# Cross attention on one core: product 7 of y in blocks in five batches, and T4 by a ScalarE copy and accumulating DMAs

## The chip, the core and the metric

The kernel runs on one NeuronCore of a Trainium2 chip. It is one program for five engines, each with its own queue that runs in order: TensorE (PE, matmuls; its weight loads are listed as PEld), VectorE (DVE), ScalarE (ACT), GpSimd (POOL) and SyncE (SP, which here only issues DMAs). ACT and POOL also issue DMAs. The metric is the device time of one execution in microseconds, as the median of several; the profile is of one further execution.

## The reference

For each of B = 8 batches, with x1 and x2 of 512 channels and 1024 positions, all in float32:

```
q = einsum('bcn,dc->bnd', x1, Wq) + bq
k = einsum('bcn,dc->bdn', x2, Wk) + bk[:, None]
v = einsum('bcn,dc->bdn', x2, Wv) + bv[:, None]
attn = softmax(einsum('bnd,bdm->bnm', q, k), axis=2)
out = einsum('bcm,bnm->bcn', v, attn) + x1
```

The queries and keys have 64 channels (d), the values 512.

## The kernel before

The kernel never forms v. It uses that v·attnᵀ = Wv·(x2·E)/den + bv, where E holds the exponentials of the scores (less a maximum for each query) and den their sums. So each batch has two large products: **y = x2·E** (512 x 1024 times 1024 x 1024) and **o = Wv·y** (512 x 512 times 512 x 1024).

**Seven products in place of eight.** Each large product is cut into 2 x 2 quarters and done by the Strassen-Winograd scheme: from the quarters of the left side (x2, names `a`; 11, 12, 21, 22) come four sums S1 to S4, from those of the right side (E, or y) come T1 to T4, and seven quarter products, numbered 1 to 7, replace eight. For y, a quarter product is 8 matmuls of 128x512 (two row halves j, four steps of 128 positions), and the profile counts two records for each float32 matmul. `multiply` does one whole (matmuls at L322), adding in PSUM onto chains in two pairs of banks, `a0`/`a1` and `c0`/`c1`. After products 1, 6 and 5 of y ScalarE copies the state of the chain from PSUM to SBUF (L333; tiles `u1`, `u6`, `u5`), because several results need it. The order of the products is 1, 2, 6, 5, 7, 3, 4. Then `evict_y` makes the four quarters of y: it adds bank and tile (step 1, L481) and multiplies with the reciprocal sums `rden` (step 2, L483).

**Products in blocks.** Some of the seven are themselves done by the same scheme one level down: product 2 (`multiply_2`, in b > 0), 3 and 4 (`multiply_onto`, in all batches). `inner_left` (L354, four additions of 128x256 on VectorE, tiles `aI`) and `inner_right` (L365, four of 128x512, tiles `eI`) make the inner sums; `inner_product` (L372) does one of seven block products with 2 matmuls of 128x256, four records. The block products that go straight into the bank of the outer chain are 2, 4 and 3. The others run in a chain of their own in a bank of the pool `ps_s`, which has two buffers and which the scores use as well; ScalarE copies what is needed to `d` and `v` (L381, 128x256). `complete` (L441) adds v to the second half of d; then d is added where the outer product belongs: for product 4 to `u6` (L451), for product 3 into y12 while bank a is read (L461).

**The order.** The order of every queue is written out by hand: `period(s, n, nn, nnn)` is one batch `s`, and into it are laid the next batch's scores, maxima and exponentials (`n`) and the queries and keys of the one after (`nn`). What matters here, as the program issues it in the middle of a period:

1. `multiply_2` on PE; on VectorE the sum over the exponentials' tiles of the second half, POOL's all-reduce of it (`total`, L235) and a small DMA (L237), then product 2's additions (L416).
2. `sum_t4` (two additions of 128x1024, L271, on VectorE), S4, T3 (L271 again), and product 6 on PE.
3. The right blocks of product 4 from T4 and the left blocks of product 3.
4. The next batch's scores for the first half of the queries (L190; copies to SBUF at L197 and L199), the queries of the batch after (L148), then the maxima over them on VectorE (`fold`, L210, L225) and POOL's all-reduce of the maximum (`highest`, L230).
5. `shares`: the reciprocals (L243), spread by two DMAs of POOL (L245, L247).
6. Product 5; the maximum is subtracted (`lower`, L258, VectorE), the exponential taken (L262, ScalarE), a first tile copied (L539) and the other three added by accumulating DMAs of POOL (`add_tile`, L531).
7. Product 3's right blocks, product 7, product 4's left blocks, product 3, and the readings of the banks: y22 from bank c, y12 from bank a.
8. The scores of the second half (the third of four tiles goes into bank a, `ps_sa`), the keys, product 4, and then o with its seven products.

Batch b = 6 has no queries of a later batch at step 4, and the last batch, b = 7, has no next batch at all. Tiles with one tag share one buffer: a new tile may be written when the old one has no readers left.

The sums of the scheme are set by short tables, for the left side in `left_sums` and `LEFT`, for the right side in `right_sums` and `RIGHT`:

```
"S1": ("21", "22", ALU.add),
"S2": ("S1", "11", ALU.subtract),
"S3": ("11", "21", ALU.subtract),
"S4": ("12", "S2", ALU.subtract),
x, y = {"T1": ("12", "11"), "T2": ("22", "T1"), "T3": ("22", "12"), "T4": ("21", "T2")}[k]
```

Of the kernel before, what the change touches and what calls it, by code (L numbers as in the profile page):

```python
# [15 lines left out]
def kernel(  # L16
# [8 lines left out]
    bv: bass.AP,  # L25
    out: bass.AP,
):

# [69 lines left out]
    def left_sums(a, *ks):  # L100

        for k in ks:
            x, y, op = {
                "S1": ("21", "22", ALU.add),
                "S2": ("S1", "11", ALU.subtract),
                "S3": ("11", "21", ALU.subtract),
                "S4": ("12", "S2", ALU.subtract),
            }[k]
            nc.vector.tensor_tensor(a["21" if k == "S3" else k], a[x], a[y], op)
            if k == "S3":  # L110
                a["S3"] = a["21"]
# [155 lines left out]

    def right_sums(t, k):

        x, y = {"T1": ("12", "11"), "T2": ("22", "T1"), "T3": ("22", "12"), "T4": ("21", "T2")}[k]  # L270
        nc.vector.tensor_tensor(t[k], t[x], t[y], ALU.subtract)  # L271

    def open_t(s):
        for n in ("T1", "T2"):
# [3 lines left out]
        s.t["T3"] = s.t["12"]  # L278

    def sum_t4(s):  # L280
        s.t["T4"] = sb.tile([P, MH, H], F32, tag="eT4", name=f"eT4_{s.b}")
        sum_e(s, "T4")

    def sum_e(s, *ks):
        for i in (0, 2):
            part = {n: v[:, i : i + 2, :] for n, v in s.t.items()}
            for k in ks:
                right_sums(part, k)
# [18 lines left out]
        4: ("22", "T4", "c", False),  # L307
    }

    def multiply(s, stage, i, left, right, n_k, last=False):  # L310


        ka, kb, bank, opens = MULT[i]
        for j in range(2):
            if opens:
                s.bank[bank, j] = ps_a.tile(
                    [P, H], F32, tag=f"{bank}{j}", name=f"ps_{stage}{bank}{j}_{s.b}_{i}"
                )
            ps = s.bank[bank, j]
            for n in HALVES if last and j else (slice(0, H),):  # L320
                for k in range(n_k):
                    nc.tensor.matmul(  # L322
                        ps[:, n],
                        left[ka][:, k, ts(j, P)],
                        right[kb][:, k, n],
                        start=opens and k == 0,
                        stop=i in (2, 3, 4) and k == n_k - 1,
                        skip_group_check=True,
                    )
            if i in (1, 6, 5):  # L330
                if j == 0:
                    s.tmp[i] = sb.tile([P, 2, H], F32, tag=f"u{i}", name=f"u{stage}{i}_{s.b}")
                nc.scalar.copy(s.tmp[i][:, j, :], ps)  # L333

    LEFT = (
        ("S1", "21", "22", ALU.add),
        ("S2", "S1", "11", ALU.subtract),
        ("S3", "11", "21", ALU.subtract),
        ("S4", "12", "S2", ALU.subtract),
    )  # L340
    RIGHT = (
        ("T1", "12", "11", ALU.subtract),
        ("T2", "22", "T1", ALU.subtract),
        ("T3", "22", "12", ALU.subtract),
        ("T4", "21", "T2", ALU.subtract),
    )

    def inner_left(s, i, x, tag):

        v = {f"{p + 1}{q + 1}": x[:, ts(q, MH // 2), ts(p, P)] for p in range(2) for q in range(2)}  # L350
        sums = sb.tile([P, 4, MH // 2, P], F32, tag=tag, name=f"aI{i}_{s.b}")
        for z, (k, x, y, op) in enumerate(LEFT):
            v[k] = sums[:, z]
            nc.vector.tensor_tensor(v[k], v[x], v[y], op)  # L354
        s.inner[i] = v

    def inner_right(s, i, x, tag):

        v = {
            f"{q + 1}{r + 1}": x[:, ts(q, MH // 2), ts(r, H // 2)] for q in range(2) for r in range(2)  # L360
        }
        sums = sb.tile([P, 4, MH // 2, H // 2], F32, tag=tag, name=f"eI{i}_{s.b}")
        for z, (k, x, y, op) in enumerate(RIGHT):
            v[k] = sums[:, z]
            nc.vector.tensor_tensor(v[k], v[x], v[y], op)  # L365
        s.inner[i, "t"] = v

    def inner_product(s, i, z, ps, opens, *copies):

        ka, kb, _, _ = MULT[z]  # L370
        for k in range(MH // 2):
            nc.tensor.matmul(  # L372
                ps,
                s.inner[i][ka][:, k, :],
                s.inner[i, "t"][kb][:, k, :],
                start=opens and k == 0,
                stop=z in (2, 3, 4) and k == MH // 2 - 1,
                skip_group_check=True,
            )
        for copy in copies:  # L380
            nc.scalar.copy(copy, ps)  # L381
# [35 lines left out]

        return evict

    def multiply_onto(s, i, d_tag, v_tag):  # L420

        b0, b1 = (s.bank[MULT[i][2], j] for j in range(2))
        chain, third = inner_bank(s, i, 0), inner_bank(s, i, 2)
        d = sb.tile([P, 2, 2, H // 2], F32, tag=d_tag, name=f"d{i}_{s.b}")
        v = sb.tile([P, 2, H], F32, tag=v_tag, name=f"v{i}_{s.b}")[:, 0, left]
        for z, ps, opens, *copies in (
            (1, chain, True, d[:, 0, 0, :]),
            (7, third, True, v),  # L430
            (6, chain, False, d[:, 1, 0, :]),
            (2, b0[:, left], False),
            (5, chain, False, d[:, 0, 1, :], d[:, 1, 1, :]),
            (4, b1[:, left], False),
            (3, b0[:, right], False),
        ):
            inner_product(s, i, z, ps, opens, *copies)

        def complete():
            both = v.unsqueeze(1).to_broadcast([P, 2, H // 2])  # L440
            nc.vector.tensor_tensor(d[:, 1], d[:, 1], both, ALU.add)  # L441

        return d.rearrange("p j a n -> p j (a n)"), complete

    def multiply_4(s):

        d, complete = multiply_onto(s, 4, "u5", "r")
        complete()
        for j in range(2):
            u6 = s.tmp[6][:, j, :]  # L450
            nc.vector.tensor_tensor(u6, u6, d[:, j, :], ALU.add)  # L451

    def multiply_3(s):

        d, complete = multiply_onto(s, 3, "u1", "r")

        def evict():
            complete()
            s.y["12"] = y = sb.tile([P, 2, H], F32, tag="y12", name=f"y12_{s.b}")
            for j in (1, 0):  # L460
                nc.vector.tensor_tensor(y[:, j, :], s.bank["a", j], d[:, j, :], ALU.add)  # L461

        return evict
# [4 lines left out]
    def evict_y(s, k, steps=(1, 2)):  # L468

        bank, add = RESULT[k]  # L470
        rden = s.rden.get(int(k[1]) - 1)
        if 1 in steps:
            s.y[k] = sb.tile([P, 2, H], F32, tag=f"y{k}", name=f"y{k}_{s.b}")
        y = s.y[k]
        for step in steps:
            for j in range(2):
                ps = s.bank.get((bank, j))
                if add is None and step == 1:
                    nc.vector.tensor_tensor(y[:, j, :], ps, rden, ALU.mult)
                elif step == 1:  # L480
                    nc.vector.tensor_tensor(y[:, j, :], ps, s.tmp[add][:, j, :], ALU.add)  # L481
                else:
                    nc.vector.tensor_tensor(y[:, j, :], y[:, j, :], rden, ALU.mult)  # L483

# [45 lines left out]
    def add_tile(s, h, i):  # L530
        nc.gpsimd.dma_start(s.mx[h], s.e[h][:, :, i, :], accum_op=ALU.add)  # L531

    def start_sum(s, h):

        e = s.e[h]
        s.mx[h] = f = sb.tile([P, 2, H], F32, tag="fold", name=f"sum_{s.b}_{h}", bufs=2)
        nc.scalar.copy(f, e[:, :, 0, :])  # L539
        for i in range(1, MH if s.b > 1 else 2):  # L540
            add_tile(s, h, i)

# [95 lines left out]
    def period(s, n, nn, nnn):  # L638

        def first(i):
            multiply(s, "y", i, s.a, s.t, MH)

        def second(i):
            multiply(s, "o", i, w, s.y, 2, n is None and i == 3)
# [31 lines left out]
        if n:  # L678
            load_a(n, "21", "22")
        first(6)  # L680
        if s.b:
            inner_right(s, 4, s.t["T4"], "eT2")
            inner_left(s, 3, s.a["S4"], "aI3")

        def next_queries():
            queries(nn)
# [14 lines left out]
            inner_right(s, 4, s.t["T4"], "eT2")  # L701
            inner_left(s, 3, s.a["S4"], "aI3")
        shares(s, 1)
        first(5)
        if s.b == 0:
            inner_right(s, 3, s.t["22"], "eT1")
            for i in range(MH):
                lower(n, 0, i)
        elif n:
            for i in range(MH):  # L710
                exponentials(n, 0, i)
            start_sum(n, 0)
        if s.b:
            inner_right(s, 3, s.t["22"], "eT1")
        first(7)
        if s.b > 1:
            inner_left(s, 4, s.a["22"], "a12")
        evict_3 = multiply_3(s)
        if s.b:
            evict_y(s, "22", (1,))  # L720
            evict_3()
        else:
            evict_3()
            evict_y(s, "22", (1,))
        for k in ("11", "12", "22"):
            evict_y(s, k, (2,))
        if s.b == 1:
# [102 lines left out]
```

## Time and profile before

| what | value |
|---|---|
| median of 3 runs | 695.88 us (695.44 to 695.99) |
| the profiled execution, its own time | 695.9 us |
| its span, first to last instruction | 694.1 us |
| granted TensorE clock | 1.000 |
| ACT busy | 254.8 us (37%) |
| POOL busy | 183.8 us (26%) |
| DMA moved | 102.72 MB, mean 148 GB/s |

The page counts busy time as the time in which an engine has at least one instruction in work. Matmuls are pipelined, so their rows overlap, and the distance between the starts of two rows tells more than a row's length. In a timeline a line is: start, length, engine, line of the code, operation, written and read tiles, shape, number of merged instructions, and in brackets the idle time before it with what ended it. Each period of b = 1 to 5 takes 84.4 to 84.5 us; that of b = 6 runs from 541.74 to 620.21, and the last begins there.

### The profile page before, as it was taken

What the parts mean: (1) busy time and instruction counts of PE and PEld (TensorE: products, weight loads), DVE (VectorE), ACT (ScalarE), POOL (GpSimd) and SP (SyncE); (2) the same over time, 40 slices, a digit from 0 to 9 for tenths busy, and PEclk for the clock granted to TensorE, in tenths of its full rate; (3) what the DMA queues carried; (4) which work ended last, traced back from release to release, by engine and by line L of the source; (5) the groups of instructions that cost most, each with busy time, mean ns of one, the idle gap of its engine ahead of it and who ended that gap; (6) DMA issues with size and microseconds to landing.
All of it is one profiled execution on the core that took longest, in us unless ns stands there. A gap on an engine that the chain in (4) does not pass through costs nothing.

```text
span 694.1 us, 6354 instructions
## 1 busy us (share of the span) xinstructions
PE 686.3 (99%) x2172; PEld 352.4 (51%) x2172; DVE 605.7 (87%) x756; ACT 254.8 (37%) x401; POOL 183.8 (26%) x135
## 2 busy tenths in 40 slices
PE   8999999999999999999999999999999999999997
PEld 4333554535545455454644546454554545545563
DVE  0999999988999879998789977999698998999684
ACT  2733353145242543234442344423444135231120
POOL 0124113512323124222162222322225222423000
PEclk9999999999999999999999999999999999999999
DMA  9676266953568463865639467384642933369103
GB/s 331 229 233 228 55 182 127 264 155 76 183 130 219 138 118 138 166 183 151 114 134 198 147 172 186 67 182 141 178 90 49 198 103 65 72 118 251 27 1 121
DMA packets 41392, 102.72 MB, mean 148 GB/s; under 512 B 4624, under 2 KB 4880, under 8 KB 41360
## 3 DMA queue, kind: packets, MB, share of 16 engines
q1 hardware_dynamic: 24256, 70.13, 29.7%
q0 software_dynamic: 15696, 29.96, 25.3%
q10 hardware_dynamic: 1408, 2.23, 1.0%
q8 instruction: 17, 0.28, 0.2%
q14 instruction: 15, 0.12, 0.1%
HBM read 72.62 MB, written 16.81 MB: 129 GB/s over the span
## 4 chain that ended last, share of the span: by engine, by line
PE 93%; DVE 3%; DMA 1%; ACT 1%; issue 1%; SPq 0%; POOL 0%; DVEq 0%; ACTq 0%
PE ps_ya L322 22%; PE ps_oa L322 16%; PE ps_i L372 14%; PE ps_oc L322 12%; PE ps_yc L322 8%; PE ps_s L190 6%; PE ps_k L148 4%; PE ps_q L148 4%; PE ps_ya L372 3%; PE ps_yc L372 3%; DMA x_head<-in_x_dram 1%; PE ps_sc L190 1%; PE ps_sa L190 1%; DVE eT L271 1%; DVE max L210 1%
## 5 line engine op out<-in xcount | busy, mean ns | idle before, releaser
L322 PE MATMUL ps_ya<-eT,aS 128*128 128x512 f32 x256 | 113.2, 596 | 0.0
L333 ACT COPY uy<-ps_ya 128x512 f32<-128x512 f32 x48 | 28.0, 587 | 163.8 <-PE ps_ya L322 152.7
L258 DVE TENSOR_TENSOR e<-e,top 128x1024 f32<-128x1024 f32 x60 | 69.8, 1217 | 10.9 <-POOL top L230 10.9
L322 PEld LDWEIGHTS ps_ya<-eT,aS 128*128 128x128 f32 x256 | 48.0, 190 | 60.8 <-issue 58.7
L235 POOL PARTITION_ALL_REDUCE den<-sum x16 | 66.3, 4141 | 44.0 <-DVE sum L225 39.0
L230 POOL PARTITION_ALL_REDUCE top<-max x16 | 31.3, 1959 | 160.6 <-DVE max L225 87.4
L262 ACT ACTIVATE e<-e 128x1024 f32<-128x1024 f32 x60 | 61.4, 1054 | 24.3 <-DVE e L258 22.7
L372 PE MATMUL ps_i<-eI,aI 128*128 128x256 f32 x276 | 66.1, 380 | 0.7 <-ACT sum L539 0.4
L322 PE MATMUL ps_yc<-e,a 128*128 128x512 f32 x144 | 63.4, 593 | 0.0
L322 PE MATMUL ps_oa<-yT,w_S 128*128 128x512 f32 x128 | 57.6, 593 | 0.0
L322 PE MATMUL ps_oc<-y,w 128*128 128x512 f32 x128 | 57.5, 592 | 0.0
L322 PE MATMUL ps_ya<-e,a 128*128 128x512 f32 x128 | 56.3, 593 | 0.0
L372 PEld LDWEIGHTS ps_i<-eI,aI 128*128 128x128 f32 x276 | 51.8, 190 | 9.0 <-ACT sum L539 0.8
L199 ACT COPY e<-ps_s 128x1024 f32<-128x1024 f32 x46 | 45.7, 1028 | 20.3 <-PE ps_s L190 17.9
L333 ACT COPY uo<-ps_oa 128x512 f32<-128x512 f32 x48 | 27.9, 584 | 62.4 <-PE ps_oa L322 55.0
L190 PE MATMUL ps_s<-q,k 64*128 64x512 f32 x188 | 47.3, 608 | 1.6 <-ACT k L172 0.8
L271 DVE TENSOR_TENSOR eT<-e,eT 128x1024 f32<-128x1024 f32 x32 | 45.5, 1442 | 0.5
L322 PEld LDWEIGHTS ps_yc<-e,a 128*128 128x128 f32 x144 | 27.3, 190 | 34.7 <-issue 32.6
L527 POOL DMA_DIRECT2D uo<-in_x_dram x21 | 25.0, 1189 | 72.4 <-DVE uo L524 67.0
L531 POOL DMA_DIRECT2D sum<-e x21 | 25.7, 1224 | 68.8 <-DMA sum<-e 54.2
L381 ACT COPY d<-ps_i 128x256 f32<-128x256 f32 x64 | 22.3, 374 | 57.5 <-PE ps_i L372 57.5
L322 PEld LDWEIGHTS ps_ya<-e,a 128*128 128x128 f32 x128 | 24.3, 190 | 30.9 <-issue 29.6
(115 smaller groups left out, 1100.5 us busy)
## 6 DMA issues: line engine op xcount, KB each, us to landing
x_in_x_dram<-in_x_dram SPq DMA_DIRECT2D x60, 512.0 KB, 6.1
a<-in_x2T_dram SPq DMA_DIRECT2D x32, 512.0 KB, 6.4
sum<-e POOLq DMA_DIRECT2D x21, 512.0 KB, 5.0
uo<-in_x_dram POOLq DMA_DIRECT2D x21, 512.0 KB, 6.3
out_dram<-uo SPq DMA_DIRECT2D x21, 512.0 KB, 4.7
x_head<-in_x_dram SPq DMA_DIRECT2D x8, 512.0 KB, 7.9
den<-row POOLq DMA_DIRECT2D x16, 256.0 KB, 3.7
r<-in_x_dram POOLq DMA_DIRECT2D x7, 512.0 KB, 6.4
```

The costliest lines, as they stand in the source:

```text
L148: nc.tensor.matmul(ps[r, :], w_sb[:, c, :], s.x[:, c, ts(h, H)], start=(c == 0), stop=(c == CT - 1),)
L190: nc.tensor.matmul(ps[g], s.k[r, ts(i, P)], s.q[r, ts(h, H)], start=True, stop=True)
L199: nc.scalar.copy(e[:, :, i, :], whole)
L230: nc.gpsimd.partition_all_reduce(s.top[h], s.mx[h][:, 0, :], P, ReduceOp.max)
L235: nc.gpsimd.partition_all_reduce(s.den[h], s.mx[h][:, 0, :], P, ReduceOp.add)
L258: nc.vector.tensor_tensor(e, e, top, ALU.subtract)
L262: nc.scalar.activation(e, e, AF.Exp)
L271: nc.vector.tensor_tensor(t[k], t[x], t[y], ALU.subtract)
L322: nc.tensor.matmul(ps[:, n], left[ka][:, k, ts(j, P)], right[kb][:, k, n], start=opens and k == 0, stop=i in (2, 3, 4) and k == n_k - 1, s ...
L333: nc.scalar.copy(s.tmp[i][:, j, :], ps)
L372: nc.tensor.matmul(ps, s.inner[i][ka][:, k, :], s.inner[i, "t"][kb][:, k, :], start=opens and k == 0, stop=z in (2, 3, 4) and k == MH // 2 ...
L531: nc.gpsimd.dma_start(s.mx[h], s.e[h][:, :, i, :], accum_op=ALU.add)
```

## The change

It does three things.

**Signs.** S2 and T2 are formed with the opposite sign; their product 6 stays the same. S4 and T4 then are sums where they were differences.

**T4.** From b = 2 on (b = 6 too), T4 is no longer formed on VectorE: ScalarE copies the quarter 21 of the exponentials into T4's tile in two halves, and two accumulating DMAs of POOL add T2's halves to it. They stand in the program where `sum_t4` stood, behind product 2.

**Product 7 of y.** In b = 2 to 5 and in b = 7 (`seven`) product 7 goes through `multiply_onto`, as 3 and 4 do. It opens bank c, in the order 1, 2, 7, 6, 4, 5, 3. Its left blocks lie in the buffer of y's T4, its right blocks in two, those of y's T1 and T2; they are made behind product 3's left blocks, ahead of the folds. Its d is added to `u5` and to `u6`, two additions of 128x1024 (`add_7`). The right half of the second row then gets nothing from bank c, and `evict_y` leaves the bank out there for y22 and y21. In these batches product 4's right blocks move from ahead of the folds to behind the first reading of y22, ahead of y12's. The maximum is subtracted from all four tiles at once; the four exponentials, the copy and the accumulating DMAs are laid by hooks between ScalarE's copies of products 5, 7 and 3. In the last batch product 4's d moves to another buffer.

```diff
@@ def right_sums
+        x, y = {"T1": ("12", "11"), "T2": ("T1", "22"), "T3": ("22", "12"), "T4": ("21", "T2")}[k]
+        nc.vector.tensor_tensor(t[k], t[x], t[y], ALU.add if k == "T4" else ALU.subtract)
@@ def sum_t4
+        s.t["T4"] = t4 = sb.tile([P, MH, H], F32, tag="eT4", name=f"eT4_{s.b}")
+        if s.b < 2:
+            sum_e(s, "T4")
+            return
+        for i in (0, 2):
+            nc.scalar.copy(t4[:, i : i + 2, :], s.t["21"][:, i : i + 2, :])
+        for i in (0, 2):
+            nc.gpsimd.dma_start(t4[:, i : i + 2, :], s.t["T2"][:, i : i + 2, :], accum_op=ALU.add)
@@ def multiply, after the copy to u
+                if hook and j == 0:
+                    hook()
@@ def multiply_onto
+        for z in (1, 2, 7, 6, 4, 5, 3) if opens else (1, 7, 6, 2, 5, 4, 3):
+            inner_product(s, i, z, *steps[z])
+            if z in hooks:
+                hooks[z]()
@@
+    def multiply_7(s, hooks):
+
+        d, complete = multiply_onto(s, 7, "i2", "y12", hooks)
+
+        def add():
+            complete()
+            for k in (5, 6):
+                nc.vector.tensor_tensor(s.tmp[k], s.tmp[k], d, ALU.add)
+
+        return add
@@ def evict_y
+        alone = 7 in s.inner and add in (5, 6)
         for step in steps:
             for j in range(2):
+                if step == 1:
+                    ps, n = s.bank[bank, j], left if alone and j else slice(0, H)
+                    nc.vector.tensor_tensor(y[:, j, n], ps[:, n], s.tmp[add][:, j, n], ALU.add)
+                elif alone and j:
+                    for x, n in ((y, left), (s.tmp[add], right)):
+                        nc.vector.tensor_tensor(y[:, j, n], x[:, j, n], rden[:, n], ALU.mult)
@@ def period
+        seven = 2 <= s.b < B - 2 or n is None
...
         first(6)
+        if s.b and not seven:
+            inner_right(s, 4, s.t["T4"], "eT2")
         if s.b:
-            inner_right(s, 4, s.t["T4"], "eT2")
             inner_left(s, 3, s.a["S4"], "aI3")
+        if seven:
+            inner_left(s, 7, s.a["S3"], "yT4")
+            inner_right(s, 7, s.t["T3"], "yT1", "yT2")
...
+        if seven:
+            hooks = [{}, {}]
+            if n:
+                for i in range(MH):
+                    lower(n, 0, i)
+                hooks = [
+                    {
+                        1: lambda: copy_first(n, 0),
+                        6: lambda: add_exponential(1),
+                        5: lambda: add_exponential(2),
+                    },
+                    {6: lambda: add_exponential(3)},
+                ]
+            first(5, (lambda: exponential(n, 0, 0)) if n else None)
             inner_right(s, 3, s.t["22"], "eT1")
             inner_left(s, 4, s.a["22"], "a12")
+            add_7 = multiply_7(s, hooks[0])
+            add_7()
+            evict_3 = multiply_3(s, hooks[1])
             evict_y(s, "22", (1,))
+            inner_right(s, 4, s.t["T4"], "eT2")
             evict_3()
```

More of the change, by code (lines that the diff above doesn't have):

```diff
@@ L104, in left_sums @@
                 "S1": ("21", "22", ALU.add),
-                "S2": ("S1", "11", ALU.subtract),
+                "S2": ("11", "S1", ALU.subtract),
                 "S3": ("11", "21", ALU.subtract),
-                "S4": ("12", "S2", ALU.subtract),
+                "S4": ("12", "S2", ALU.add),
             }[k]
@@ L268, in right_sums @@
     def right_sums(t, k):
-        x, y = {"T1": ("12", "11"), "T2": ("22", "T1"), "T3": ("22", "12"), "T4": ("21", "T2")}[k]
-        nc.vector.tensor_tensor(t[k], t[x], t[y], ALU.subtract)
+        x, y = {"T1": ("12", "11"), "T2": ("T1", "22"), "T3": ("22", "12"), "T4": ("21", "T2")}[k]
+        nc.vector.tensor_tensor(t[k], t[x], t[y], ALU.add if k == "T4" else ALU.subtract)
     def open_t(s):
@@ L280, in sum_t4 @@
     def sum_t4(s):
-        s.t["T4"] = sb.tile([P, MH, H], F32, tag="eT4", name=f"eT4_{s.b}")
-        sum_e(s, "T4")
+        s.t["T4"] = t4 = sb.tile([P, MH, H], F32, tag="eT4", name=f"eT4_{s.b}")
[6 more added lines that the diff above has]
+            nc.gpsimd.dma_start(t4[:, i : i + 2, :], s.t["T2"][:, i : i + 2, :], accum_op=ALU.add)
     def sum_e(s, *ks):
@@ L308, with multiply @@
     }
-    def multiply(s, stage, i, left, right, n_k, last=False):
+    def multiply(s, stage, i, left, right, n_k, last=False, hook=None):
         ka, kb, bank, opens = MULT[i]
@@ L333, in multiply @@
                 nc.scalar.copy(s.tmp[i][:, j, :], ps)
+                if hook and j == 0:
+                    hook()
     LEFT = (
         ("S1", "21", "22", ALU.add),
-        ("S2", "S1", "11", ALU.subtract),
+        ("S2", "11", "S1", ALU.subtract),
         ("S3", "11", "21", ALU.subtract),
-        ("S4", "12", "S2", ALU.subtract),
+        ("S4", "12", "S2", ALU.add),
     )
@@ L342 @@
         ("T1", "12", "11", ALU.subtract),
-        ("T2", "22", "T1", ALU.subtract),
+        ("T2", "T1", "22", ALU.subtract),
         ("T3", "22", "12", ALU.subtract),
-        ("T4", "21", "T2", ALU.subtract),
+        ("T4", "21", "T2", ALU.add),
     )
@@ L355, in inner_left, with inner_right @@
         s.inner[i] = v
-    def inner_right(s, i, x, tag):
+    def inner_right(s, i, x, *tags):
         v = {
@@ L361, in inner_right @@
         }
-        sums = sb.tile([P, 4, MH // 2, H // 2], F32, tag=tag, name=f"eI{i}_{s.b}")
+        shape = [P, 4 // len(tags), MH // 2, H // 2]
+        sums = [sb.tile(shape, F32, tag=t, name=f"eI{i}{t}_{s.b}") for t in tags]
         for z, (k, x, y, op) in enumerate(RIGHT):
-            v[k] = sums[:, z]
+            v[k] = sums[z // shape[1]][:, z % shape[1]]
             nc.vector.tensor_tensor(v[k], v[x], v[y], op)
@@ L418, in multiply_2, with multiply_onto @@
         return evict
-    def multiply_onto(s, i, d_tag, v_tag):
-        b0, b1 = (s.bank[MULT[i][2], j] for j in range(2))
+    def multiply_onto(s, i, d_tag, v_tag, hooks={}):
+        bank, opens = MULT[i][2:]
+        if opens:
+            for j in range(2):
+                s.bank[bank, j] = ps_a.tile([P, H], F32, tag=f"{bank}{j}", name=f"ps_y{bank}{j}_{s.b}_{i}")
+        b0, b1 = (s.bank[bank, j] for j in range(2))
         chain, third = inner_bank(s, i, 0), inner_bank(s, i, 2)
-        d = sb.tile([P, 2, 2, H // 2], F32, tag=d_tag, name=f"d{i}_{s.b}")
+        d = sb.tile([P, 2, 2, H // 2], F32, tag=d_tag, name=f"d{i}_{s.b}", bufs=1 + (d_tag == "a21"))
         v = sb.tile([P, 2, H], F32, tag=v_tag, name=f"v{i}_{s.b}")[:, 0, left]
[L428 to L437, printed above, removed]
+        steps = {
+            1: (chain, True, d[:, 0, 0, :]),
+            7: (third, True, v),
+            6: (chain, False, d[:, 1, 0, :]),
+            2: (b0[:, left], opens),
+            5: (chain, False, d[:, 0, 1, :], d[:, 1, 1, :]),
+            4: (b1[:, left], opens),
+            3: (b0[:, right], False),
+        }
+        for z in (1, 2, 7, 6, 4, 5, 3) if opens else (1, 7, 6, 2, 5, 4, 3):
+            inner_product(s, i, z, *steps[z])
+            if z in hooks:
+                hooks[z]()
         def complete():
@@ L445, in multiply_4 @@
     def multiply_4(s):
-        d, complete = multiply_onto(s, 4, "u5", "r")
+        d, complete = multiply_onto(s, 4, "u5" if s.b < B - 1 else "a21", "r")
         complete()
@@ L451, in multiply_4, with multiply_3 @@
             nc.vector.tensor_tensor(u6, u6, d[:, j, :], ALU.add)
-    def multiply_3(s):
-        d, complete = multiply_onto(s, 3, "u1", "r")
+    def multiply_7(s, hooks):
[5 more added lines that the diff above has]
+        return add
+    def multiply_3(s, hooks):
+        d, complete = multiply_onto(s, 3, "u1", "r", hooks)
         def evict():
@@ L474, in evict_y @@
         y = s.y[k]
+        alone = 7 in s.inner and add in (5, 6)
         for step in steps:
             for j in range(2):
[L477 to L481, printed above, removed]
+                if step == 1:
[4 more added lines that the diff above has]
+                        nc.vector.tensor_tensor(y[:, j, n], x[:, j, n], rden[:, n], ALU.mult)
                 else:
@@ L531, in add_tile, with copy_first @@
         nc.gpsimd.dma_start(s.mx[h], s.e[h][:, :, i, :], accum_op=ALU.add)
+    def copy_first(s, h):
+        s.mx[h] = sb.tile([P, 2, H], F32, tag="fold", name=f"sum_{s.b}_{h}", bufs=2)
+        nc.scalar.copy(s.mx[h], s.e[h][:, :, 0, :])
     def start_sum(s, h):
-        e = s.e[h]
-        s.mx[h] = f = sb.tile([P, 2, H], F32, tag="fold", name=f"sum_{s.b}_{h}", bufs=2)
-        nc.scalar.copy(f, e[:, :, 0, :])
+        copy_first(s, h)
         for i in range(1, MH if s.b > 1 else 2):
@@ L638, in period, with first @@
     def period(s, n, nn, nnn):
-        def first(i):
-            multiply(s, "y", i, s.a, s.t, MH)
+        seven = 2 <= s.b < B - 2 or n is None
+        def first(i, hook=None):
+            multiply(s, "y", i, s.a, s.t, MH, hook=hook)
         def second(i):
@@ L680, in period, with add_exponential @@
         first(6)
+        if s.b and not seven:
+            inner_right(s, 4, s.t["T4"], "eT2")
         if s.b:
-            inner_right(s, 4, s.t["T4"], "eT2")
             inner_left(s, 3, s.a["S4"], "aI3")
+        if seven:
+            inner_left(s, 7, s.a["S3"], "yT4")
+            inner_right(s, 7, s.t["T3"], "yT1", "yT2")
+        def add_exponential(i):
+            exponential(n, 0, i)
+            add_tile(n, 0, i)
         def next_queries():
@@ L703, in period @@
         shares(s, 1)
-        first(5)
-        if s.b == 0:
-            inner_right(s, 3, s.t["22"], "eT1")
[L707 to L716, printed above, removed]
+        if seven:
[12 more added lines that the diff above has]
+            first(5, (lambda: exponential(n, 0, 0)) if n else None)
+            inner_right(s, 3, s.t["22"], "eT1")
             inner_left(s, 4, s.a["22"], "a12")
-        evict_3 = multiply_3(s)
-        if s.b:
+            add_7 = multiply_7(s, hooks[0])
+            add_7()
+            evict_3 = multiply_3(s, hooks[1])
             evict_y(s, "22", (1,))
+            inner_right(s, 4, s.t["T4"], "eT2")
             evict_3()
         else:
-            evict_3()
-            evict_y(s, "22", (1,))
+            first(5)
+            if s.b == 0:
+                inner_right(s, 3, s.t["22"], "eT1")
+                for i in range(MH):
+                    lower(n, 0, i)
+            else:
+                for i in range(MH):
+                    exponentials(n, 0, i)
+                start_sum(n, 0)
+                inner_right(s, 3, s.t["22"], "eT1")
+            first(7)
+            if s.b > 1:
+                inner_left(s, 4, s.a["22"], "a12")
+            evict_3 = multiply_3(s, {})
+            if s.b:
+                evict_y(s, "22", (1,))
+                evict_3()
+            else:
+                evict_3()
+                evict_y(s, "22", (1,))
         for k in ("11", "12", "22"):
```

## The prediction

> **What bounds the kernel now.** I read the shares of busy time first, then the chain that ended last, then the timelines of TensorE (PE), VectorE (DVE), ScalarE (ACT) and GpSimd (POOL) through one whole period (b = 3) and through the period that differs (b = 6). Batches are counted from 0; change and code give product 7 its new form for b = 2 to 5 and 7.
>
> ```profile
> PE 686.3 (99%) x2172; PEld 352.4 (51%) x2172; DVE 605.7 (87%) x756; ACT 254.8 (37%) x401; POOL 183.8 (26%) x135
> ...
> PE 93%; DVE 3%; DMA 1%; ACT 1%; issue 1%; SPq 0%; POOL 0%; DVEq 0%; ACTq 0%
> ```
>
> PE sets the end, but DVE has only a few microseconds of slack in a period. So less PE work is worth its full time only where DVE, ACT and DMA still deliver on time. PE in period 3 (start, length of the merged row, number of records):
>
> ```profile
> 322.41 7.03 PE L322 MATMUL ps_yc<-e,a 128*128 128x512 f32 x16
> 329.28 1.03 PE L372 MATMUL ps_i<-e,aS 128*128 128x256 f32 x4
> ...
> 335.41 1.99 PE L190 MATMUL ps_s<-q,k 64*128 64x512 f32 x8
> 337.23 1.02 PE L190 MATMUL ps_sa<-q,k 64*128 64x512 f32 x4
> ```
>
> Row lengths overlap (a mean of 593 ns is not the price of a matmul), so I go from start to start. Product 7 takes 16 records from 322.41 to 329.28: 6.87 us. Product 3, in blocks already, takes 28 records from 329.28 to 335.41: 6.13, of which 0.09 is the step to the scores (product 2 in blocks, 295.22 to 301.26, takes 6.04). There is no idle time in these rows. DVE at the same place:
>
> ```profile
> 328.75 1.49 DVE L481 TENSOR_TENSOR y<-ps_yc,uy 128x512 f32<-128x512 f32 x2
> 334.47 0.69 DVE L441 TENSOR_TENSOR d<-d,v 128x512 f32<-128x512 f32 x1 [4.23 <-ACT d L381]
> 335.27 1.29 DVE L461 TENSOR_TENSOR y<-ps_ya,d 128x512 f32<-128x512 f32 x2
> ```
>
> DVE waits 4.23 us for product 3's copies, then frees bank a at 336.56; the scores write that bank (ps_sa) at 337.23. The cover is 0.67 us. I keep it in mind.
>
> **Part 1, product 7 in blocks: PE.** 6.87 - 6.04 = 0.83 us removed per place; five places, 4.1 us if all of it showed.
>
> **Part 2, what DVE does for it (b = 2 to 5).** Start-to-start durations from period 3. Removed: T4's two additions, 2.27 us. Added ahead of the folds: seven's left blocks 1.46 and right blocks 2.53 (rows L354, L365). Moved behind: product 4's right blocks, 2.53. Before the folds DVE so runs 2.27 - 1.46 = 0.81 earlier, and the lowering begins at 319.4 instead of 320.20; its four rows, product 3's right blocks and product 4's left blocks (8.55 from 320.20 to 328.75) end at 327.9. Next in its queue is product 7's completion, which needs the copies of inner product 5. A block product of 4 records takes 0.863 (334.46 after 333.59), and 5 is the sixth in the new order: PE starts it at 322.41 + 5 x 0.863 = 326.73, its two copies start 1.06 later (as 330.34 follows 329.28) and end at 328.44. From 328.47 DVE has in its queue, ahead of the release of bank a: the completion 0.60; two additions of 128x1024 onto u5 and u6, 2 x 1.14; the rows of y22, 0.60 and a half one 0.34; product 4's right blocks 2.54; product 3's completion 0.80; its two rows of y12, 0.61 + 0.68. Sum 8.45, end 336.92. A matmul follows such a release by 0.15 (580.35 to 580.49 below). So ps_sa starts at 337.07 and not at 337.23 - 0.83 = 336.40: **the saving is 0.16 per period, not 0.83**; the old 4.23 us of waiting are filled with 8.45 us of work. What is queued behind (y's multiplications, T1, T2, the folds) is 0.36 later; the completion of product 4 has 0.85 of idle time before it (347.93), which covers that. Bounds for one place: -0.3 (a DVE row stretched) to 0.83 (if the queue were short).
>
> **Part 3, exponentials between copies (b = 2 to 5).** Four exponentials (1.05 each) and the copy of 1.03 do not change in number; they stand between copies for which PE waits. In my schedule ACT gets: exponential 0 at 320.65 to 321.7, before u5's second copy at 322.6; the copy of the sum 323.84 to 324.87, then v's copy at 325.2; exponential 1 326.43 to 327.49, before the copies at 327.79; exponential 2 328.44 to 329.50, product 3's first copy due at 329.6. Each fits, by 0.1 to 0.9 us. Product 3 waits some 0.15 for the last copy of the bank that it reuses; it is inside the wait for DVE. Price taken: 0; if one slipped, up to 1.05 per period. The accumulating DMAs of the sum are issued 0.8 earlier than at 328.35.
>
> **Part 4, the last batch.** No folds and no scores stand behind product 3. DVE: completion from 652.9, to 655.8 with u5 and u6, y22 to 656.8, product 4's right blocks to 659.3 (its third one by 658.7, needed by PE at 659.8), y21 by 671.7 (needed at 671.85). Saving: 0.83 in full, with 0.1 to 1 us of cover.
>
> **Part 5, T4 by ACT and DMA, b = 2 to 7.** ACT: two copies of 128x1024, 1.03 each, in idle time of 4.79 us (before 304.90; likewise before 558.28): nothing. POOL: two DMAs of 512 KB behind the all-reduce and its small DMA. In b = 2 to 5 and 7 nobody needs T4 for 20 us: nothing. In **b = 6 product 7 stays whole and product 4's right blocks stay where they were, straight behind T3, in front of the folds.** There DVE will stand at its queue's head, waiting for the second DMA. Rows of b = 6, DVE, PE, POOL:
>
> ```profile
> 555.26 4.69 DVE L271 TENSOR_TENSOR eT<-e,eT 128x1024 f32<-128x1024 f32 x2
> 559.87 1.21 DVE L109 TENSOR_TENSOR aS<-a,aS 128x1024 f32<-128x1024 f32 x1
> ...
> 563.27 0.68 DVE L365 TENSOR_TENSOR eI<-eT 128x512 f32<-128x512 f32 x1
> ...
> 567.27 1.22 DVE L210 TENSOR_TENSOR max<-e 128x1024 f32<-128x1024 f32 x1
> ...
> 579.66 0.68 DVE L365 TENSOR_TENSOR eI<-e 128x512 f32<-128x512 f32 x1
> ```
>
> ```profile
> 579.08 1.03 PE L372 MATMUL ps_i<-e,aS 128*128 128x256 f32 x4
> 580.49 1.97 PE L372 MATMUL ps_i<-eI,aI 128*128 128x256 f32 x8 [0.39 <-ACT sum L539]
> ```
>
> ```profile
> 559.02 0.55 POOL L237 DMA_DIRECT2D few<-den  x1 [0.30 <-POOL den L235]
> ...
> 580.74 1.24 POOL L531 DMA_DIRECT2D sum<-e  x1 [4.34 <-ACT d L381]
> 586.61 1.19 POOL L531 DMA_DIRECT2D sum<-e  x1 [4.63 <-DMA sum<-e]
> ```
>
> The reader is to see that PE already waits for DVE here: product 3's second step needs the third right block, which ends at 579.66 + 0.68 = 580.35, and PE starts at 580.49, 0.55 late (the row names ACT's sum, but the block is the operand). So from the folds on every microsecond that DVE loses is one that PE loses. Without T4's sums DVE reaches the blocks at 561.0 (the 2.35 of collision with the all-reduce then falls on S4). T4's first DMA can be issued at 559.6. Nearest row: the same accumulation between two SBUF tiles of 512 KB:
>
> ```profile
> sum<-e POOLq DMA_DIRECT2D x21, 512.0 KB, 5.0
> ```
>
> These come one at a time. While one moves, the windows of 1 us from 582 to 586 show 92, 193, 188 and 68 GB/s, with the engines' share above 1 in the middle ones: full. Two must share, so the second lands 512 KB / 193 GB/s = 2.7 later: 559.6 + 5.0 + 2.7 = 567.3. Then the four right blocks and three's left blocks, 4.0 (563.27 to 567.27): the folds start at 571.3, **4.0 us late, and PE with them**.
>
> [...] The row shows 5.0 for this very operation, so I take 4.0 and keep 0.5 to 5 as ends. [...]
>
> [...] PE would be idle here from about 580.1 to 584.5. The slices of granted clock are all at 9 or above and no idle stretch of the trace before is that long, so no run here shows it. [...]
>
> **Sum.** -4 x 0.16 - 0.83 + 4.0 = +2.5 us. The profiled execution took 695.9 (span 694.1, 1.8 around it), the median 695.88, so no correction is needed: **698.4 us**, 0.36% slower. A measurement tells no change from one of about 0.2% (1.4 us).
>
> **Rivals.**
> - *T4 lands early in b = 6* (the other side). Place: product 4's right blocks behind T3. For it: the DMA engines are idle from 561 on, and 4 KB rows may be cheaper than the 2 KB of the sum. Against: the 193 GB/s. [...] Chance 0.15.
> - *The saving shows in full in b = 2 to 5*: some of DVE's 8.45 us proves to lie elsewhere. -4.1 + 4.0: 695.8, no change. Against: DVE's queue is in order. Chance 0.10; together with the first rival 691.9 to 692.5, 0.08.
> - *ACT slips*: an exponential stands in front of a copy for which PE waits, 1.05 in each of four periods in place of the saving: 698.4 + 4 x 1.2 = 703, or half of that. For it: margins of 0.1 to 0.3 at two places. Chance 0.13.
> - Forecast 0.54, with the clock drop inside it.
>
> Faster takes the 0.08 and half of the first rival: 0.16; same 0.20 (the other half, the second rival, small misses of the forecast); slower 0.64. Range 694.9 to 701.0: it holds the forecast with the clock drop (700.1), the first two rivals and half of the third.
>
> **What would show it.** In b = 6 a DVE wait of about 6 us at L365's first row after T3, named by T4's DMA, and PE idle about 4.5 before product 3's second step. In b = 2 to 5 no wait of DVE before product 3's completion, and one of about 0.7 of PE before ps_sa, ended by DVE's rows of y12; periods of 84.3 instead of 84.46. In b = 7 a period shorter by 0.8. The forecast is wrong if T4 lands by 564, or if ps_sa starts without a wait.

## The result, and the profile after

| kernel | median | ratio to before, 95% interval | profiled execution | its span |
|---|---|---|---|---|
| before | 695.91 us | | 695.9 us | 694.1 us |
| changed | 701.8 us (701.07 to 702.86) | 1.0083 (1.007 to 1.0095) | 701.28 us | 699.5 us |

The changed kernel is 0.83% slower. Each of its four executions is slower than each of the four before. The start of TensorE's first product in each batch cuts the execution into periods:

| period | before | changed |
|---|---|---|
| b = 1 | 84.46 | 84.46 |
| b = 2 to 5 | 84.46, 84.46, 84.46, 84.47 | 84.40, 84.40, 84.40, 84.39 |
| b = 6 | 78.47 | **85.03** |
| b = 7, to the end | 73.91 | 72.99 |

Everything that was lost was lost in one period, b = 6, in which product 7 is not even touched. The shares of busy time and the granted clock (40 slices, in tenths) of the changed kernel's page:

```profile
PE 685.5 (98%) x2232; PEld 365.0 (52%) x2232; DVE 622.4 (89%) x809; ACT 276.0 (39%) x438; POOL 201.4 (29%) x147
...
PEclk9999999999999999999999999999999998999999
```

PE has 60 records more than before (12 in each of five places) and is yet busy 0.8 us less; DVE has 16.7 us more, ACT 21.2. One slice of the clock shows 8, and that slice lies in b = 6. (The lines of the code moved: L365 is now L377, L372 is L384, L381 is L393, L461 is L493, L258 is L259; T4's copies are L288, its DMAs L290.) The timelines of period 6, DVE, then POOL, then PE:

```profile
555.01 3.17 DVE L110 TENSOR_TENSOR aS<-a,aS 128x1024 f32<-128x1024 f32 x1
558.10 2.35 DVE L272 TENSOR_TENSOR e<-e 128x1024 f32<-128x1024 f32 x2
567.43 0.69 DVE L377 TENSOR_TENSOR eI4eT<-eT 128x512 f32<-128x512 f32 x1 [6.98 <-DMA eT<-eT]
...
571.44 1.22 DVE L211 TENSOR_TENSOR max<-e 128x1024 f32<-128x1024 f32 x1
...
583.83 0.68 DVE L377 TENSOR_TENSOR eI3eT<-e 128x512 f32<-128x512 f32 x1
```

```profile
558.39 0.56 POOL L238 DMA_DIRECT2D few<-den  x1 [0.29 <-POOL den L236]
559.14 1.77 POOL L290 DMA_DIRECT2D eT<-eT  x2 [0.20 <-issue]
```

```profile
578.83 1.03 PE L384 MATMUL ps_i<-e,aS 128*128 128x256 f32 x4
584.66 3.75 PE L384 MATMUL ps_i<-eI3eT,aI 128*128 128x256 f32 x8 [4.80 <-ACT sum L570]
588.20 1.42 PE L384 MATMUL ps_ya<-e,aS 128*128 128x256 f32 x4
```

Three things are to be seen. DVE stands idle for 6.98 us at product 4's first right block, until T4's DMA lands (567.31). From there on it is late: the folds begin at 571.44, where they began at 567.27, and product 3's third right block ends at 583.83 + 0.68 = 584.51. PE starts on it at 584.66, after 4.80 us of idling; counted from start to start it waits 4.96 us, where it had waited 0.55. And then its eight records take 3.75 us where they took 1.97. The same period by stretches (length, then busy time and in brackets the instructions of PE, PEld, DVE, ACT and POOL, the granted clock, the share of the DMA engines and GB/s):

```profile
541.49:579.70 38.21, 38.21 (x113) 19.44 (x111) 27.84 (x34) 11.30 (x18) 10.09 (x9) 1.00 0.60 146
579.70:584.60 4.90, 0.16 (x1) 0.00 (x0) 4.87 (x7) 4.67 (x6) 0.56 (x1) 0.75 0.26 54
584.60:589.00 4.40, 4.34 (x10) 3.54 (x11) 3.15 (x7) 1.02 (x4) 1.22 (x1) 0.50 0.59 101
```

PE does nothing between 579.9 and 584.6, the clock goes down in that stretch, and the next 4.4 us run at half of it. By the clock's own record it was at one half from 582.17 to 588.99. Against their usual distance of 0.216 us the records in it are 2.15 us late in all, which is half of the 4.33 us that PE worked at half clock.

In period 3 the place that matters is the third tile of scores:

```profile
334.89 0.68 DVE L462 TENSOR_TENSOR d<-d,v 128x512 f32<-128x512 f32 x1
335.67 1.29 DVE L493 TENSOR_TENSOR y<-ps_ya,d 128x512 f32<-128x512 f32 x2
```

```profile
334.54 1.99 PE L191 MATMUL ps_s<-q,k 64*128 64x512 f32 x8
337.01 1.13 PE L191 MATMUL ps_sa<-q,k 64*128 64x512 f32 x4 [0.49 <-DVE y L493]
```

DVE's completion of product 3 has no idle time before it any more (it had 4.23 us), bank a is free at 336.96, and PE, which comes to the scores 0.87 us earlier than before (334.54), waits for it. Start to start the wait is 0.65 us.

### The profile page after: what moved, and what is told of

It reads as the page before. It is cut to its first block, busy times and chain, and to the rows that moved or that the text cites. A ratio compares the mean times of both kernels' runs of the same rounds, so it can differ in the third digit from the quotient of the medians.

```text
span 699.5 us, 6607 instructions
## 1 busy us (share of the span) xinstructions
PE 685.5 (98%) x2232; PEld 365.0 (52%) x2232; DVE 622.4 (89%) x809; ACT 276.0 (39%) x438; POOL 201.4 (29%) x147
## 5 line engine op out<-in xcount | busy, mean ns | idle before, releaser
L236 POOL PARTITION_ALL_REDUCE den<-sum x16 | 72.7, 4545 | 43.2 <-DVE sum L226 38.2
L259 DVE TENSOR_TENSOR e<-e,top 128x1024 f32<-128x1024 f32 x60 | 69.8, 1216 | 11.0 <-POOL top L231 11.0
L263 ACT ACTIVATE e<-e 128x1024 f32<-128x1024 f32 x60 | 62.8, 1059 | 29.3 <-DVE e L259 27.9
L393 ACT COPY d<-ps_i 128x256 f32<-128x256 f32 x84 | 29.3, 374 | 46.9 <-PE ps_i L384 46.4
L331 PEld LDWEIGHTS ps_oa<-yT,w_S 128*128 128x128 f32 x128 | 24.3, 190 | 30.8 <-issue 30.1
L331 PEld LDWEIGHTS ps_oc<-y,w 128*128 128x128 f32 x128 | 24.4, 190 | 30.6 <-issue 29.1
L211 DVE TENSOR_TENSOR max<-max,e 128x1024 f32<-128x1024 f32 x30 | 36.8, 1225 | 3.4 <-DVE max L211 0.5
L558 DVE SCALAR_TENSOR_TENSOR uo<-ps_oc,bv_sb,uo 128x512 f32<-128x512 f32 x42 | 30.6, 745 | 8.5 <-PE ps_oc L331 8.5
L517 DVE TENSOR_TENSOR y<-y,den 128x512 f32<-128x512 f32 x54 | 33.7, 682 | 0.0
```

Of the source, the lines that this page charges most:

```text
L211: nc.vector.tensor_tensor(f, e[:, :, 0, :] if i == 1 else f, e[:, :, i, :], op)
L236: nc.gpsimd.partition_all_reduce(s.den[h], s.mx[h][:, 0, :], P, ReduceOp.add)
L259: nc.vector.tensor_tensor(e, e, top, ALU.subtract)
L263: nc.scalar.activation(e, e, AF.Exp)
L331: nc.tensor.matmul(ps[:, n], left[ka][:, k, ts(j, P)], right[kb][:, k, n], start=opens and k == 0, stop=i in (2, 3, 4) and k == n_k - 1, s ...
L558: nc.vector.scalar_tensor_tensor(o[:, j, :], s.bank[bank, j], bias(j), o[:, j, :], ALU.add, ALU.add)
```

## The experiments

Each kernel ran with the kernel before on the same chip; all ratios are to that. In the code cuts `...` marks what is left out. **Theory A**: in b = 6 DVE waits in order for T4's DMA, PE waits for DVE, and PE's idling lowers its clock. **Theory A'**: in b = 2 to 5 the saving of product 7 is taken by DVE's queue ahead of the release of bank a. **Rival B**: the loss comes from product 7 in blocks. **Rival C**: the accumulating DMAs disturb as such. **Rival D**: the low clock has another cause than the idling.

**1. T4 in b = 6 on VectorE.**

```diff
-        if s.b < 2:
+        if s.b < 2 or s.b == B - 2:
             sum_e(s, "T4")
```

> Edit: in batch 6 alone T4 is formed by VectorE's two additions, as before the change; all else as changed. Theory A (VectorE waits in batch 6 for T4's DMA, TensorE waits for VectorE, and the idle stretch lowers the clock): period 6 falls from 85.0 us to the old 78.5, TensorE has its old wait of 0.55 there and no more, the clock is 1.000 again, and the time is 694.7 us, 1.2 below the kernel before. Rival B (the slowdown comes from product 7 in blocks in the other periods): it stays at 700 or above.

Measured: 694.78 us, ratio 0.9983 (0.9976 to 0.9991). Period 6 takes 77.85 us, b = 2 to 5 84.39 to 84.40, the last 72.99. PE's row at the place of the old wait:

```profile
579.11 1.03 PE L384 MATMUL ps_i<-e,aS 128*128 128x256 f32 x4
579.98 1.89 PE L384 MATMUL ps_i<-eI3eT,aI 128*128 128x256 f32 x8
```

So rival B is out: with product 7 in blocks in five batches and T4 as before in this one batch, the kernel is slightly faster than before. One detail was missed: period 6 was expected at the old 78.5 with its wait of 0.55 us, and that wait is gone too. In this execution POOL's all-reduce began 0.74 us earlier than in the profile of before (554.80 against 555.54), relative to nearly the same DVE times. T4's two additions, beside which it runs in both, overlapped it for less time (555.29 to 557.98, before 555.54 to 558.72) and took 3.92 us and not 4.69; DVE came to the folds at 566.52.

**2. T4 by DMA in b = 6, its reader moved.**

```diff
-        if s.b and not seven:
+        if s.b == 1:
             inner_right(s, 4, s.t["T4"], "eT2")
...
                 evict_y(s, "22", (1,))
+                if s.b > 1:
+                    inner_right(s, 4, s.t["T4"], "eT2")
                 evict_3()
```

> Edit: T4 in batch 6 stays with ScalarE and the DMAs, but product 4's right blocks, which read it, move there too behind the reading of y22 (in batches 2 to 5 and 7 they are there already). Theory A: the DMA itself costs nothing, only the place of its reader does. VectorE reaches the folds 4.8 us earlier than in the kernel before, the wait of 4.96 us is gone and the old one of 0.55 with it: 694.1 us. Rival C (the accumulating DMAs themselves disturb, by loading the DMA engines or POOL): a good part of the 6.5 us of period 6 stays, above 698.

Measured: 694.38 us, ratio 0.9976 (0.9967 to 0.9986); period 6 takes 77.85 us. DVE's timeline there:

```profile
562.27 0.42 DVE L365 TENSOR_TENSOR aI<-aS,aI 128x256 f32<-128x256 f32 x1
564.99 1.23 DVE L211 TENSOR_TENSOR max<-e 128x1024 f32<-128x1024 f32 x1 [2.30 <-ACT e L200]
...
581.26 0.68 DVE L377 TENSOR_TENSOR eI4eT<-eT 128x512 f32<-128x512 f32 x1
```

DVE comes to the folds so early that it waits for the scores, and the right blocks at 581.26 find T4 long landed (567.50). PE's second step of product 3 starts at 580.05, 0.87 after the first, with no wait. The DMAs are the same two; only the place of their reader differs. Rival C is out.

**3. The idle stretch filled.** Five matmuls of 128x512 that nobody reads, into the unused half of a tile of the pool `ps_s`, behind product 3's first inner product in b = 6:

```diff
...
             inner_product(s, i, z, *steps[z])
+            if s.b == B - 2 and i == 3 and z == 1:
+                for _ in range(5):
+                    nc.tensor.matmul(pair[:, 1, :], s.a["22"][:, 0, 0:P], s.t["22"][:, 0, :], start=True, stop=True)
```

> Edit: in batch 6, behind the first inner product of product 3, five matmuls of 128x512 whose results nobody reads are laid into TensorE's idle stretch (4.3 us of work in 4.8 us of waiting). Theory A with the clock: VectorE's wait for T4 and the start of product 3's second step stay where they were, but the clock stays at 1.000, and the time falls by the 2.1 us that half the clock cost: 699.3 us. Rival D (the low clock is not caused by the idle stretch): the half clock is there again and the time stays at 701 to 702.

Measured: 699.12 us, ratio 1.0044 (1.0032 to 1.0056), 2.7 below the changed kernel's median and 2.4 between the two profiled executions. The same stretches:

```profile
580.10:584.40 4.30, 4.30 (x11) 1.91 (x11) 4.27 (x6) 4.09 (x5) 0.02 (x1) 1.00 0.25 61
584.40:589.00 4.60, 4.60 (x23) 4.03 (x22) 3.05 (x8) 1.39 (x4) 1.20 (x1) 1.00 0.67 114
```

```profile
580.14 4.46 PE L461 MATMUL ps_i<-e,a 128*128 128x512 f32 x10
584.43 1.89 PE L384 MATMUL ps_i<-eI3eT,aI 128*128 128x256 f32 x8
```

DVE still waits for T4 (6.07 us), product 3's second step still starts only at 584.43, its eight records take 1.89 us in place of 3.75, and the clock stays at 1.00. More work for PE made the kernel faster, and rival D is out. Period 6 takes 82.14 us, 2.89 less than in the changed kernel's profile. Not all of that is the clock: T4 landed 0.98 us earlier after the period's start in this execution, and the fillers hold PE some 0.3 beyond the point at which it could have gone on. What is left for the clock is 2.2, near the 2.15 read from the rows above.

**4. T4 by DMA alone, product 7 whole.**

```diff
-        seven = 2 <= s.b < B - 2 or n is None
+        seven = False
...
```

> Edit: product 7 whole in all batches, its old order with it; T4 by ScalarE and DMAs from batch 2 on, product 4's right blocks straight behind T3 in all of them. Theory A: in batches 2 to 5 VectorE waits for T4 too, some 5 us, and the folds start 3 us late, but TensorE has 3.1 us more to do there (the queries), so product 3's second step just finds its blocks: periods of 84.5, and only batch 6 loses its 6.5 us: 702.4 us. Rival B: 695.9 us, since product 7 is whole.

Measured: 707.54 us (703.77 to 713.9), ratio 1.017 (1.0133 to 1.0207). Worse than expected by 5 us, with executions 10 us apart: the mechanism is there, but the cover in b = 2 to 5 does not reach. In b = 2 DVE waits 7.48 us for T4 (first issue 222.99, second landing 230.71), and PE waits at product 3's second step:

```profile
230.83 0.69 DVE L377 TENSOR_TENSOR eI4eT<-eT 128x512 f32<-128x512 f32 x1 [7.48 <-DMA eT<-eT]
248.06 1.97 PE L384 MATMUL ps_i<-eI3eT,aI 128*128 128x256 f32 x8 [1.80 <-ACT sum L570]
```

Start to start, PE's wait there is 1.97 us in b = 2, then 0.30, 1.32 and 1.15 in b = 3 to 5, and 5.18 in b = 6, again with half clock after it (PE worked 3.4 us at it; the mean clock of this execution is 0.998). The 3.1 us of the queries were too little cover. In the changed kernel the same blocks stand later in b = 2 to 5, as a part of the edit for product 7, and DVE has no such wait there: by this and by experiment 2 it is their place that makes T4's DMA free of cost. (Product 7 is whole here as well, so this run alone does not part the two.)

**5. Product 7 in blocks alone, T4 on VectorE.**

```diff
-        if s.b < 2:
+        if s.b >= 0:
             sum_e(s, "T4")
```

> Edit: product 7 in blocks as changed, but T4 by VectorE's two additions in all batches. Theory A': in batches 2 to 5 VectorE has 2.27 us more ahead of the folds than in the changed kernel, so it comes to product 7's completion 2.07 us later than its operands are there (0.16 of waiting stands there in the changed kernel), bank a is freed 2.07 later and periods 2 to 5 take 86.5 us in place of 84.4; batch 6 is free of its wait: 694.8 + 4 x 2.07 = 703.1 us. Rival E (T4's additions are hidden, as VectorE waits anyway): 694.8, as with T4 on VectorE in batch 6 alone.

Measured: 703.99 us, ratio 1.0116 (1.0101 to 1.0132). PE waits at ps_sa 2.29, 2.25, 2.29 and 1.92 us in b = 2 to 5, each time for DVE's reading of bank a. In b = 2:

```profile
254.66 1.13 PE L191 MATMUL ps_sa<-q,k 64*128 64x512 f32 x4 [2.13 <-DVE y L493]
257.04 4.84 PE L149 MATMUL ps_k<-x_in_x_dram,wqk_sb 128*64 128x512 f32 x16
```

The periods are 87.69, 86.00, 86.04 and 85.67 us, the first with 3.4 us at half clock (256.05 to 259.46; the mean clock of this execution is 0.997) behind its wait; in the other three, after waits nearly as long, the clock stayed full. T4's additions are not hidden: in the places that the change gave to DVE's work, product 7 in blocks costs time without T4's DMA, some 1.3 to 1.6 us per period (2.07 was expected), and the clock besides.

**6. Bank a first.** In the batches with product 7 in blocks, product 4's right blocks go behind y12:

```diff
-            inner_right(s, 4, s.t["T4"], "eT2")
             evict_3()
+            inner_right(s, 4, s.t["T4"], "eT2")
```

> Edit to the changed kernel: in batches 2 to 5 and 7 product 4's right blocks (2.5 us of VectorE) move from ahead of y12's reading of bank a to behind it. Theory A': bank a is freed when product 3's copies allow it, near 335.7 in period 3, before the scores want it (336.3); the wait of 0.65 us at ps_sa and the 0.1 of its restart go, periods of 83.65 in place of 84.40, while batch 6 keeps its loss: 698.8 us. Rival F (the saving of product 7 is lost elsewhere, in ScalarE's copies and exponentials): no more than 0.3 us in all, 701.5.

Measured: 702.74 us, ratio 1.0095 (1.0079 to 1.011): not the 698.8 expected. The periods tell why. b = 2 to 5 take 83.63, 83.67, 83.64 and 83.67 us, as expected, with no wait at ps_sa. So the saving of product 7 was not lost in ScalarE's copies. But the last takes 75.54 and not 72.99, period 6, whose loss varies from execution to execution, 86.21, and b = 1 begins 0.74 later in this execution. I had moved the blocks in the last batch as well, where product 4 follows product 3 at once.

**7. Both places.** Experiments 2 and 6 together.

> Edit: the two places together: product 4's right blocks behind y12's reading in batches 2 to 5 and 7, and in batch 6 behind the reading of y22, ahead of y12's. Theory A and A' add up: 694.4 - 4 x 0.75 = 691.4 us, 4.6 below the kernel before, which is what five times 0.83 and the old wait of 0.55 in batch 6 come to. If the two are not independent it stays above 693.

Measured: 695.47 us (694.03 to 696.55), ratio 0.999 (0.9983 to 0.9997), and not the 691.4 expected. Periods of 83.63 to 83.68, 77.98 in b = 6, and again 75.53 in the last. PE there:

```profile
655.71 1.03 PE L384 MATMUL ps_i<-eT,a 128*128 128x256 f32 x4
659.02 1.97 PE L384 MATMUL ps_i<-eI4eT,aI 128*128 128x256 f32 x8 [2.28 <-DVE eI4eT L377]
```

The two gains add up, and my own misplacement takes 2.45 of them away. Of the 18 executions, eight lie near 694.2 us with a mean clock of 0.999 to 1.000, nine near 696.0 with 0.997 or 0.998, and one at 695.21 between them. The profiled one is of the first group.

**8. Both places, the last batch as the change had it.**

```diff
...
+            if n is None:
+                inner_right(s, 4, s.t["T4"], "eT2")
             evict_3()
-            inner_right(s, 4, s.t["T4"], "eT2")
+            if n:
+                inner_right(s, 4, s.t["T4"], "eT2")
...
```

> Edit: as e7_both, but in the last batch product 4's right blocks stay ahead of y12's reading, where the change put them. There product 4 follows product 3 at once, with no scores and keys between, and in e7_both it waited 2.45 us for its blocks. Theory A': the last period takes 73.0 us again in place of 75.5 and the other periods stay at 83.65: 694.4 - 2.5 = 691.9 us, 4.1 below the kernel before. If the order of the last batch is not the cause, it stays near 694.4.

Measured: **691.71 us** (691.6 to 692.02), ratio **0.9937** (0.9925 to 0.995). Periods 83.67, 83.67, 83.67, 83.64, 77.97, 73.00. The scores in period 3:

```profile
334.26 1.99 PE L191 MATMUL ps_s<-q,k 64*128 64x512 f32 x8
336.08 1.02 PE L191 MATMUL ps_sa<-q,k 64*128 64x512 f32 x4
```

No wait, and the row of ps_sa is 1.02 long again and not 1.13. This version beats both kernels: the change's savings were real, and two places of the same four VectorE instructions had used them up.

**9. The last batch's wait filled.** Experiment 7 with its wait of 2.45 us, into which two unread matmuls of 128x512 are laid, as in experiment 3.

> Edit: as e7_both with its wait of 2.45 us in the last batch left in place, and two matmuls of 128x512 without a reader (1.7 us) laid into it. The 18 runs of e7_both fell into two groups, near 694.2 us at a mean clock of 1.000 and near 696.0 at 0.997. Theory A with the clock: these are executions in which the wait did or did not bring the clock to one half for 3.4 us (1.7 us lost); filled, all executions lie near 694.2. Rival D: the two groups have another cause and are there again.

Measured: 694.35 us (693.82 to 694.58), ratio 0.9976 (0.9965 to 0.9986), all eight executions at a mean clock of 0.999 or 1.000. The upper group is gone, so here too it was the wait that lowered the clock, in some executions and not in others. (Experiment 7 ran on another chip, beside its own runs of before.)

**10. T4 on VectorE with bank a first.** Experiment 8 with the edit of experiment 5.

> Edit: as e8_both_last_kept, with T4 by VectorE's two additions in all batches. It asks what T4's way by ScalarE and DMA is worth once bank a is read first. Theory A': VectorE comes 2.07 us late to product 7's completion, as in e5_seven_alone, but with product 4's right blocks out of the way bank a is free near 336.6 in period 3, wanted at 336.3 to 336.7; with the restart and a late copy of u5 that is about 0.5 us per period, 693.7 us in all. Rival: the DMA way is needed in full, 2.1 us per period as in e5_seven_alone: 700.

Measured: 692.91 us (691.82 to 694.56), ratio 0.9961 (0.9947 to 0.9975). The periods are 83.75, 83.64, 83.96 and 84.07; the small waits are 0.14 and 0.24 us in product 7 itself. Once bank a is read first, T4's way over ScalarE and POOL is worth little: 0.7 us between this profile and that of experiment 8 (692.59 against 691.88), 1.2 between the medians, no longer the 1.3 to 1.6 us per period of experiment 5. The two ran on different chips and their intervals touch, so even this much is not certain.

## Why the prediction was wrong, step by step

The direction and the chain from T4's DMA over DVE to PE were right, the size was not: +2.5 us forecast, +5.4 between the profiled executions, +5.9 between the medians, outside the range.

| term of the sum | forecast | measured |
|---|---|---|
| b = 2 to 5, four times | -0.64 | -0.26 |
| b = 6, PE's wait for DVE | +4.0 | +4.41 (4.96 less the old 0.55) |
| b = 6, the clock | 0, only in the range | **+2.15** |
| last batch | -0.83 | -0.92 |
| sum | +2.5 | +5.4 |

- **The step that failed is to leave the clock out of the sum** and count it in the range alone. The prediction had the idle stretch right in place and nearly in length (580.1 to 584.5 forecast, 579.9 to 584.66 measured). No run shows the 1.7 us by which its 700.1 lies above 698.4; the clock cost 2.15 here. The trace shows the clock halved 2.3 us after PE's last matmul (582.17 against 579.86), and for 6.83 us. In each of the three profiled executions with this wait unfilled (4.96 us here, 5.18 and 6.54 in experiments 4 and 6, start to start; mean clocks 0.994, 0.998 and 0.994) the clock was halved, so it belonged into the sum, at 1.6 to 2.2 us: half of the 3.3 to 4.33 us that PE worked at half clock here and in experiments 4 to 6. Experiment 3 shows it by itself. The clock is 2.15 of the 2.9 us that the sum missed; it alone would have given 700.6, still within the range. The rest is the next two terms, some 0.4 each, and executions slower than the profiled one.
- **T4's landing was right**: the second DMA landed at 567.31, forecast 567.3 from the accumulation's row. In part that is luck: the first was issued 0.46 earlier than assumed, and the second landed 8.2 us after that issue in place of 7.7. PE's schedule was 0.25 earlier than before by then, so the wait came out 0.4 longer. No run shows the early landing behind the range's lower end, 694.9, and behind the loss of 0.5 us kept as an end: DVE waited 6.98 us for T4 here, 6.07 in experiment 3 and 7.48 in b = 2 of experiment 4.
- **The queue ahead of bank a was right**: ps_sa starts 14.65 us after product 7 does, forecast 14.66. But the saving was booked as 0.16 and is 0.06: the row of ps_sa is 1.13 us long in place of 1.02, and the step from its first matmul to the second is 0.10 longer. Over four periods that is 0.4 us.
- **ScalarE's slots were right**: in period 3 the copies of products 7 and 3 stand behind waits for PE in ACT's rows, not behind exponentials (the one without such a wait, at 329.47, starts 1.07 us after its product, as the first at 323.43 does), and the rival of slipping exponentials did not show.
- **The last batch was right** (0.92 with what lies behind it).
- The other rivals: T4 did not land early; the saving in b = 2 to 5 did not show in full. Both were ruled out by the trace, and experiments 2 and 8 show what each would have been worth if the order had allowed it.

Not settled: the loss in b = 6 differs from execution to execution (701.07 to 702.86, and 86.21 against 85.03 us in experiment 6). PE waited 6.54 us in that profile and 4.96 in this one. The traces say where the 1.58 between them arose: counted from the period's start, T4's first DMA was issued 2.08 us later there (19.74 against 17.66), and the second landed 0.5 sooner after that issue. Of the 2.08, 1.67 is there already at DVE's reciprocals (L244; 7.33 against 5.66), for which POOL's small DMA (L246) ahead of its all-reduce and of T4's DMAs waits. In experiment 3 the issue came within 0.1 of the changed kernel's, and the landing 0.9 sooner after it. Why DVE and the DMAs differ so is open. Product 7 in blocks in b = 6 was not tried.

## What to carry to other kernels

When work moves to a DMA, ask first what stands behind its reader in the reader's own queue: the same two DMAs cost 7 us or nothing, and the four additions that read them cost 0.7 us per batch or nothing, by their place alone. An instruction that frees a resource for the bounding engine goes ahead of one that only prepares something for later, unless the later one follows at once, as in the last batch. And a wait of TensorE is priced with the clock that it may lose, not by its length alone: in these profiles the clock went to half after one idle stretch of 2.13 us (experiment 5), stayed full after others of 2.09, 2.13 and 2.28 (experiments 5 and 7), and was halved in the one of 4.80 (the changed kernel).

## What the runs showed of the hardware

- **In a wait of TensorE its clock was halved, for longer than the wait lasted.** In the changed kernel PE idled from 579.86 to 584.66, and its clock stood at one half from 582.17 to 588.99, 6.83 us, of which PE worked 4.33.
- **The same wait may or may not cost the clock.** Of experiment 5's idle stretches of 2.13, 2.09, 2.13 and 1.76 us only the first was followed by half clock (3.4 us). In experiment 7's profile the clock stayed full through one of 2.28 (mean 1.000), and of its 18 executions eight have a mean clock of 0.999 to 1.000 and nine, some 1.8 us slower, 0.997 or 0.998. What decides between the two is not shown.
- **In the changed kernel the price was half of the time that TensorE worked at half clock**: 2.15 us late by its records, in 4.33 us of work. PE worked 3.4 us at half clock in experiments 4 and 5 and 3.3 in experiment 6; an estimate by the same half is 1.6 to 1.7 us.
- Unread matmuls in the wait prevented it: experiment 3 ran at 1.00 in the two stretches (580.10 to 589.00) in which the changed kernel showed 0.75 and 0.50, and all eight executions of experiment 9 have a mean clock of 0.999 or 1.000.
- In the rows of ps_sa the step from the first matmul to the second is 0.53 us after a wait (changed kernel, period 3) and 0.43 without one (before). The first step of the scores (334.54 to 335.07) is 0.53 too and has no wait before it, so the wait need not be the cause.
